# A weight's last row spread by matmuls, a bias loaded in place, reloads on another DMA queue, and program order at a seam

## The chip, the core and the metric

The kernel runs on one core of a Trainium2 chip. The metric is the device time of one execution in microseconds (us), the median of several runs. A core has TensorE (PE, with its weight loads shown apart as PEld), VectorE (DVE), ScalarE (ACT), GpSimd (POOL) and SyncE (SP). SP, ACT and POOL can issue DMAs, each on a queue of its own; the transfers themselves run on 16 DMA engines that the queues share.

## The reference: two half feed-forwards around a long convolution

The input x has 8 sequences of 2048 tokens with 256 channels. Three residual sub-layers follow one another:

```python
x = x + 0.5 * ffn(layernorm(x), w1, b1, w2, b2)
x = x + s4(layernorm(x), ...)
x = x + 0.5 * ffn(layernorm(x), w1, b1, w2, b2)

ffn(x):  relu(x @ w1 + b1) @ w2 + b2            # w1 is 256 x 1024, w2 1024 x 256
s4(x):   y = causal convolution of every channel along the 2048 tokens with its own kernel K
         r = x + y + x * D
         (r - mean(r)) / sqrt(var(r) + 1e-5) * ln_w + ln_b
```

Everything is float32. In the first and last layer norm of the list above (those ahead of `ffn`) there is no scale or shift.

## The kernel before

**Numbers in two parts.** A float32 product is made on PE as three matmuls of parts: each operand is split into a high part, rounded, and a low part, the rest. So w1 and w2 are kept as pairs `w1t[0], w1t[1]` and `w2t[0], w2t[1]`, and the layer's input as `xh, xl`.

**The last row and the bias.** A normalised row sums to zero over the 256 channels, so the last channel can be dropped: `load_weights` subtracts w1's last row from every row, and the place of row 255 takes the bias b1, with the input's channel 255 set to 1.0 (a memset of `xn`'s last column). To do that it loads w1 in four quarters of 256 columns (lines 163 to 167, on SP), then the last row and the bias, each broadcast to all 128 partitions (lines 168 and 169, 512 KB of written data each, on ACT's queue), then w2 in two halves (line 172, SP). Per quarter, DVE subtracts the last row (line 177), adds the bias through a column of the identity which is 1 on partition 127 only (line 178, recorded as the helper's line 117), ACT rounds the high part (182) and DVE subtracts for the low part (183). Partition p, slot d of `raw1` holds row 128 d + p, so row 255 is on partition 127.

**FFN sub-layers.** `sublayer` (line 819 on) runs a feed-forward over 64 groups of 256 tokens. A group has 8 steps, one for each 128 of the 1024 hidden columns: `up` makes six matmuls (line 802), ACT and DVE take the relu in two parts (lines 870 and 117), `down` makes six matmuls (line 812) three steps later. A generator `pre(g)` prepares the input of a group some steps ahead (load, statistics, root, norm, transposition into `xh`, `xl`), one stage per step; `post(g, po)` adds the result and stores it. The framework may change the order of instructions on an engine by its own planned times, unless an instruction is kept in program order. `sublayer` keeps ACT and DVE in program order in its lead-in (before the first matmul step) if it has work in `first`, or if the constant `MB` is set; `first` is `load_weights()` in sub-layer a and empty in b, and `MB = 0`.

Once split, the weights are also written to DRAM (lines 198 and 199), since the S4 block uses their place in SBUF (tags `wA`, `wB`) for its states.

**The S4 block.** The convolution runs over 32 batches of 8 channels, in groups `gr` 0 to 11. The last group but two (`gr` 9) is batches 26 and 27, then come 28 and 29, and 30 and 31. `states(gr)` (matmuls of line 984) makes the states between 128-token blocks, a recurrence on DVE or POOL carries them on, and `outputs(gr)` makes the result: for every batch it loads two `tz` (line 1036; a Toeplitz matrix of the convolution kernel from `kpad`) and two `ot` (line 1054) on SP, 256 KB each; ACT copies the input into two `uc` (1043); PE makes 16 matmuls of `tz` by `uc` (line 1059, 128 rows) and 32 of `ot` by the states (1068, 64 rows, in two halves c = 0, 1 that use different rows of the array); ACT evacuates the two results into `u` (1074). The tiles of these loads are borrowed from tags of the FFN stage (`xl`, `pl`, `x`, `xh`, `xn`), so a load starts when its tile is free.

**The seam.** After the last batch in the program stand the reload of w1 for sub-layer b (line 1147, eight pieces of 256 KB on SP, into `wb1`, tag `wA`), of w2 (line 1151, four pieces of 512 KB on SP, into `wb2`, tag `wB`), and the broadcasts of ln_w and ln_b on POOL's queue (line 1160). They are issued as soon as their tiles are free, so among the loads of the last batches: those of wb1 went out between 1039.45 and 1045.5, those of wb2 from 1074.67. Then `pre_b` starts: it loads the x of a group (line 1168, SP) into one of five `x` slots, adds ln_b on POOL, takes the statistics of the convolution's rows (`st_r`, `mv_r`), the root on ACT (`s_r`), the scaled difference `ys` (1184 on, recorded at the helper's line 117), adds it to x, and goes on with a second norm (`st_fb` to `nb_fb`, `xn`) and the transposition.

Of the kernel before, what the change touches and what calls it, by code (L numbers as in the profile page):

```python
# [10 lines left out]
F32 = mybir.dt.float32  # L11
F32R = mybir.dt.float32r
# [3 lines left out]
ALU = mybir.AluOpType  # L16
# [3 lines left out]
P = 128  # L20
# [23 lines left out]
def macaron_s4d_kernel(  # L44
# [17 lines left out]
    nc = tc.nc  # L62
    V = nc.vector
    A_ = nc.scalar
    G_ = nc.gpsimd

    B, L, H = x.shape
    N = c_re.shape[1]
    W = w1.shape[1]
# [4 lines left out]
    NDC = H // P  # L74
    NFC = W // P
    NTB = 2
# [5 lines left out]
    PINW = 1  # L82
    NZ = 1
    PINF = 0
    MB = 0
    PINT = 1
    XY = 4
    NU = NFC // 2
# [16 lines left out]
    wpool = ctx.enter_context(tc.tile_pool(name="wpool", bufs=1))  # L105
# [4 lines left out]
    def bank(tag, name):  # L110
        return ps.tile([P, 512], F32, name=name, tag=tag, bufs=BANKS[tag])

    def slot(tag, shape, name, dtype=F32):
        return work.tile(shape, dtype, name=name, tag=tag, bufs=BUFS[tag])

    def stt(o, a, s, b, op0, op1):
        return V.scalar_tensor_tensor(out=o, in0=a, scalar=s, in1=b, op0=op0, op1=op1)  # L117
# [4 lines left out]
    ident = const.tile([P, P], F32, name="ident")  # L122
# [27 lines left out]
    W1Q = [nc.sync] * 4  # L150
    W2Q = [nc.sync] * 2

    def load_weights():
        for _ in range(XL):
            yield
        q = W // 4
        raw1 = room[1][:, 0 : NDC * W].rearrange("p (i d f) -> p i d f", i=4, d=NDC)
        raw2 = room[1][:, NDC * W : NDC * W + NFC * H].rearrange("p (f m) -> p f m", m=H)
        last, bias = (
            room[1][:, NDC * W + NFC * H + i * W : NDC * W + NFC * H + (i + 1) * W] for i in range(2)  # L160
        )
        w2v = w2.rearrange("(fc p) m -> p fc m", p=P)
        for i in range(4):
            fs = slice(i * q, (i + 1) * q)
            W1Q[i].dma_start(
                out=raw1[:, i], in_=w1[:, fs].rearrange("(dc p) f -> p dc f", p=P)
            )
        nc.scalar.dma_start(out=last, in_=w1[H - 1].partition_broadcast(P))
        nc.scalar.dma_start(out=bias, in_=b1.partition_broadcast(P))
        for i in range(2):  # L170
            fs = slice(4 * i, 4 * i + 4)
            W2Q[i].dma_start(out=raw2[:, fs], in_=w2v[:, fs, :])
        for _ in range(7):
            yield
        for i in range(4):
            fs = slice(i * q, (i + 1) * q)
            V.tensor_sub(
                raw1[:, i], raw1[:, i], last[:, fs].unsqueeze(1).to_broadcast([P, NDC, q])
            )
            stt(raw1[:, i, NDC - 1], bias[:, fs], ident[:, P - 1 : P], raw1[:, i, NDC - 1], ALU.mult, ALU.add)  # L180
            hi = w1t[0][:, :, fs]
            A_.copy(hi, raw1[:, i])
            V.tensor_sub(w1t[1][:, :, fs], raw1[:, i], hi.bitcast(F32))
            yield
        for _ in range(NZ):
            yield
        for i in range(4):
            fs = slice(2 * i, 2 * i + 2)
            hi = w2t[0][:, fs, :]
            for ins in (  # L190
                A_.activation(hi, raw2[:, fs], AF.Copy, scale=0.5),
                stt(w2t[1][:, fs, :], raw2[:, fs], 0.5, hi.bitcast(F32), ALU.mult, ALU.subtract),
            ):
                if i < PINW:
                    tc.keep_in_program_order(ins)
            yield
        for i in range(2):
            nc.sync.dma_start(out=w1_dram[i], in_=w1t[i].bitcast(F32))
            nc.sync.dma_start(out=w2_dram[i], in_=w2t[i].bitcast(F32))
# [700 lines left out]
    xts = {}  # L900
# [45 lines left out]
    BL = 9  # L946
    xbuf = {}
    steps = {}

    BEHIND = [BH] * (len(PLAN) - 1) + [BL]  # L950

# [76 lines left out]
    def outputs(gr):  # L1028
        xs = states_of(gr)
        for p0, bt in batches(gr):  # L1030
            py, tzs, ucs, ots = [], [], [], []
            for c in range(2):
                tz = slot(TZS[gr >= LASTX][(2 * bt + c) % 3], [P, PB, P], f"tz{bt}_{c}")

                row = kpad[BCH * bt + c, 1:]
                nc.sync.dma_start(
                    out=tz,
                    in_=bass.AP(row.tensor, row.offset, [[1, P], [2 * KROW, PB], [1, P]]),
                )
                tzs.append(tz)  # L1040

                uc = slot("hx", [P, PB, P], f"uc{bt}_{c}")
                A_.copy(
                    uc.rearrange("p l (q m) -> p l q m", q=NQ),
                    u[:, :, BCH * bt + c : BCH * (bt + 1) : 2, :].rearrange("p q l m -> p l q m"),
                )
                ucs.append(uc)
            for ri in range(2):
                tag = OTS[gr >= LASTX][(2 * bt + ri) % 4]
                ot = (  # L1050
                    slot(tag, [P, PB, P], f"ot{bt}_{ri}") if tag
                    else xn.rearrange("p i (l m) -> p (i l) m", m=P)
                )
                nc.sync.dma_start(out=ot, in_=o_dram[bt][:, ri * PB * P : (ri + 1) * PB * P])
                ots.append(ot)
            for c in range(2):
                py.append(bank("h", f"py{bt}_{c}").rearrange("p (l m) -> p l m", l=PB))
                for l in range(PB):
                    nc.tensor.matmul(
                        py[c][:, l, :], ucs[c][:, l, :], tzs[c][:, l, :],  # L1060
                        start=(l == 0), stop=False, skip_group_check=True,
                    )

            for l in range(PB):
                for ri in range(2):
                    for c in range(2):
                        cs = slice(c * N, (c + 1) * N)
                        nc.tensor.matmul(
                            py[c][:, l, :], xs[cs, ri, p0 + l, :], ots[ri][cs, l, :],
                            start=False, stop=(l == PB - 1 and ri == 1), skip_group_check=True,  # L1070
                        )
            for c in range(2):

                A_.copy(
                    uo[:, :, bt, :, c::2], py[c].rearrange("p l (q m) -> p q m l", q=NQ)
                )

    def some(j0, j1):

# [51 lines left out]
        {"half": NG // 2, "tables": NG * 3 // 4},  # L1131
    )

    for gr in (1, 2, 3):
        states(gr)
    for gr in range(len(sizes)):
# [1 line left out]
        if gr and gr + AHEAD < len(sizes):  # L1138
            states(gr + AHEAD)


    wb1 = wpool.tile([P, 2, NDC, W], F32R, name="wb1", tag="wA")
    wb2 = wpool.tile([P, 2, NFC, H], F32R, name="wb2", tag="wB")
    for f in range(0, W, W // 4):
        fs = slice(f, f + W // 4)
        for i in range(2):
            nc.sync.dma_start(out=wb1[:, i, :, fs].bitcast(F32), in_=w1_dram[i][:, :, fs])
    for f in range(0, NFC, 4):
        fs = slice(f, f + 4)
        for i in range(2):  # L1150
            nc.sync.dma_start(out=wb2[:, i, fs].bitcast(F32), in_=w2_dram[i][:, fs])

    G_.memset(xn[:, :, H - 1 : H], 1.0)
    ys = wpool.tile([P, 2, NTB, H], F32, name="ys", tag="wE")


    lnw_sb = slot("e", [P, H], "lnw_sb")
    lnb_sb = slot("te", [P, H], "lnb_sb")
    for dst, src in ((lnw_sb, ln_w), (lnb_sb, ln_b)):
        nc.gpsimd.dma_start(out=dst, in_=src.partition_broadcast(P))  # L1160

    def pre_b(g):
        by_dma = g >= DMA_B
        for _ in range(0 if by_dma else XL):
            yield
        xt = xts[g] = slot("x", [P, NTB, H], f"xb_{g}")
        i0 = g * NTB
        nc.sync.dma_start(out=xt, in_=x1_dram[i0 : i0 + NTB].rearrange("i m h -> m i h"))
        G_.tensor_add(xt, xt, lnb_sb.unsqueeze(1).to_broadcast([P, NTB, H]))  # L1169
        uc = [uo[:, i // CQ, :, i % CQ] for i in range(P - 1 - i0, P - 1 - i0 - NTB, -1)]  # L1170
        mv = stats(uc, f"r{g}", PIN & 2)
        yield
        s = root(mv, f"r{g}")
        yield
        rs = rstds(mv, s, f"r{g}")
        yield
        y = ys[:, g % 2]
        for i in range(NTB):
            yb, lb = (t.rearrange("p (b h) -> p b h", h=BCH) for t in (y[:, i, :], lnw_sb))
            stt(yb, uc[i], mv[:, i, 0:1], lb, ALU.subtract, ALU.mult)  # L1180
        yield
        for i in range(NTB):
            ins = stt(xt[:, i, :], y[:, i, :], rs[:, i : i + 1], xt[:, i, :], ALU.mult, ALU.add)
            if PIN & 1:
                tc.keep_in_program_order(ins)
        yield
        return (yield from ffn_in(xt, f"b{g}", True, by_dma))
# [46 lines left out]
```

## Time and profile before

| | us |
|---|---|
| median of 3 runs | 1843.84 |
| lowest and highest | 1843.77, 1846.55 |
| the profiled execution | 1843.95 |
| its span in the trace | 1842.2 |
| last matmul of FFN a starts, first of the S4 block | 856.6, 860.8 |
| PE idle before the first transposition of FFN b begins | 1081.9 |
| first matmul of FFN b | 1094.31 |
| mean granted PE clock | 0.98 of full |

The page is one profiled execution. Its busy rows tell how long each engine worked; a row of the 40 slices has one digit for each 46 us, 9 for 90% and more. A line of a timeline has the start in us, the length in us, engine, source line, operation, what it writes `<-` what it reads, the shape, how many; in brackets how long the engine had been idle before, and what released it. Line numbers are those of the code above; line 117 is a helper that several places call. In a windows table each row is a stretch of time, with busy time and count per engine, then the granted PE clock, the mean busy share of the 16 DMA engines, and GB/s.

Section 6 of the page lists what DMAs took from issue to landing, in the median; four of its rows:

```profile
xa<-in_L_attn_x_dram SPq DMA_DIRECT2D x64, 256.0 KB, 2.9
...
tz<-kpad SPq DMA_DIRECT2D x64, 256.0 KB, 4.2
xb<-x_dram SPq DMA_DIRECT2D x64, 256.0 KB, 2.7
```

### The profile page before, as it was taken

Reading aid. Unit: us, or ns where it says so; the run is one execution under the profiler, and the core shown is the slowest. Engines: PE = TensorE matmul, PEld = TensorE weight load, DVE = VectorE, ACT = ScalarE, POOL = GpSimd, SP = SyncE. Lnnn points to the kernel's source line nnn. Section 1 sums busy time; section 2 is a strip of 40 time slices with the busy share of each in tenths; the row PEclk is TensorE's granted clock in tenths of the full one; section 3 lists DMA queues with packets and bytes.
Section 4 is the critical chain, followed back from the end, with each engine's and each line's share of the span. In section 5 each row is a group of like instructions: output and inputs, shape, how many; then the busy total and the mean of one; then the engine's idle time right before and its main releaser. Section 6 shows DMA issues by size and latency. Waiting matters only on the chain. (4 is left out here: it accounts for less than half of the span.)

```text
span 1842.2 us, 41540 instructions
## 1 busy us (share of the span) xinstructions
PE 1747.9 (95%) x15147; PEld 1715.8 (93%) x15147; DVE 1492.6 (81%) x4919; ACT 925.2 (50%) x2139; POOL 713.7 (39%) x964
## 2 busy tenths in 40 slices
PE   6999799998998999999989879999999999999999
PEld 5999799988998999998888879999999999999998
DVE  5999897888899867765999947888888888888875
ACT  4455334554655655553545425555555555555553
POOL 1116851888587414111778612222222222222220
PEclk9999899998999999999999979999999999999999
DMA  5112132787888933334878833333332333333332
GB/s 203 47 47 56 52 111 77 241 237 227 247 250 246 247 110 90 101 105 137 253 232 235 256 115 87 93 89 92 88 100 85 91 98 87 98 89 90 94 95 55
DMA packets 299696, 246.39 MB, mean 134 GB/s; under 512 B 169954, under 2 KB 242402, under 8 KB 298978
## 3 DMA queue, kind: packets, MB, share of 16 engines
q1 hardware_dynamic: 297456, 241.75, 45.2%
q8 instruction: 119, 1.95, 0.4%
q10 hardware_dynamic: 1266, 1.31, 0.2%
q0 software_dynamic: 768, 0.66, 0.2%
q14 instruction: 87, 0.71, 0.1%
HBM read 92.93 MB, written 111.15 MB: 111 GB/s over the span
## 5 line engine op out<-in xcount | busy, mean ns | idle before, releaser
L812 PE MATMUL po_a<-wa,hx_a 128*128 128x256 f32 x3072 | 457.1, 287 | 17.4 <-DVE hx_a L117 17.1
L802 PE MATMUL ph_a<-xh_a,wa 128*128 128x256 f32 x2048 | 460.2, 289 | 5.2 <-ACT xh_a L749 3.5
L802 PE MATMUL ph_b<-xh_b,wb 128*128 128x256 f32 x2048 | 443.2, 284 | 2.5 <-ACT xh_b L749 2.4
L812 PE MATMUL po_b<-wb,hx_b 128*128 128x256 f32 x3072 | 441.2, 283 | 0.3 <-DVE hx_b L117 0.3
L812 PEld LDWEIGHTS po_a<-wa,hx_a 128*128 128x128 f32 x3072 | 407.7, 194 | 23.4 <-DVE hx_a L117 22.4
L812 PEld LDWEIGHTS po_b<-wb,hx_b 128*128 128x128 f32 x3072 | 400.5, 192 | 0.5 <-DVE hx_b L117 0.5
L802 PEld LDWEIGHTS ph_a<-xh_a,wa 128*128 128x128 f32 x2048 | 361.3, 196 | 6.8 <-ACT xh_a L749 3.9
L802 PEld LDWEIGHTS ph_b<-xh_b,wb 128*128 128x128 f32 x2048 | 352.8, 193 | 3.6 <-ACT xh_b L749 3.0
L802 PE MATMUL ph_a<-xl_a,wa 128*128 128x256 f32 x1024 | 294.1, 290 | 23.4 <-DVE xl_a L751 20.6
L870 ACT ACTIVATE hx_b<-ph_b 128x256 fp32r<-128x256 f32 x512 | 191.6, 381 | 244.3 <-PE ph_b L802 226.6
L117 DVE SCALAR_TENSOR_TENSOR hx_a<-ph_a,hx_a 128x256 fp32r<-128x256 f32 x512 | 207.9, 412 | 127.7 <-ACT hx_a L870 126.6
L870 ACT ACTIVATE hx_a<-ph_a 128x256 fp32r<-128x256 f32 x512 | 189.0, 381 | 228.8 <-PE ph_a L802 213.6
L1169 POOL TENSOR_TENSOR xb<-xb,lnb_sb 128x512 f32<-128x512 f32 x64 | 84.0, 1315 | 523.3 <-DMA xb<-x_dram 384.4
L802 PE MATMUL ph_b<-xl_b,wb 128*128 128x256 f32 x1024 | 285.2, 284 | 0.0
L117 DVE SCALAR_TENSOR_TENSOR hx_b<-ph_b,hx_b 128x256 fp32r<-128x256 f32 x512 | 210.1, 414 | 57.3 <-ACT hx_b L870 51.7
L802 PEld LDWEIGHTS ph_a<-xl_a,wa 128*128 128x128 f32 x1024 | 201.2, 196 | 27.0 <-DVE xl_a L751 23.5
L733 POOL TENSOR_TENSOR xa<-xa,hb 128x512 f32<-128x512 f32 x64 | 85.5, 1336 | 362.4 <-ACT xn L701 328.0
L802 PEld LDWEIGHTS ph_b<-xl_b,wb 128*128 128x128 f32 x1024 | 197.4, 193 | 0.2 <-DVE xl_b L751 0.2
L701 ACT ACTIVATE xn<-xa,nb_fa,t_fa 128x255 f32<-128x255 f32 x128 | 69.7, 591 | 104.2 <-DVE nb_fa L117 82.2
L733 POOL TENSOR_TENSOR xb<-xb,hb 128x512 f32<-128x512 f32 x64 | 93.9, 1467 | 50.0 <-ACT xn L701 34.5
L701 ACT ACTIVATE xn<-xb,nb_fb,t_fb 128x255 f32<-128x255 f32 x128 | 69.9, 594 | 75.7 <-DVE nb_fb L117 72.0
L761 DVE COPY pl_b<-xn 128x512 uint16<-128x512 uint16 x62 | 42.7, 688 | 74.3 <-ACT xn L701 74.3
(264 smaller groups left out, 2773.2 us busy)
## 6 DMA issues: line engine op xcount, KB each, us to landing
xa<-in_L_attn_x_dram SPq DMA_DIRECT2D x64, 256.0 KB, 2.9
x_dram<-xa SPq DMA_DIRECT2D x64, 256.0 KB, 2.3
o<-u SPq DMA_DIRECT2D x32, 512.0 KB, 4.2
pv<-planes SPq DMA_DIRECT2D x32, 512.0 KB, 3.6
pt<-u SPq DMA_DIRECT2D x32, 512.0 KB, 3.3
tz<-kpad SPq DMA_DIRECT2D x64, 256.0 KB, 4.2
xb<-x_dram SPq DMA_DIRECT2D x64, 256.0 KB, 2.7
out_dram<-xb SPq DMA_DIRECT2D x64, 256.0 KB, 2.9
```

The source lines that it names most:

```text
L117: return V.scalar_tensor_tensor(out=o, in0=a, scalar=s, in1=b, op0=op0, op1=op1)
L701: A_.activation(dst, src, AF.Identity, bias=nb[:, i : i + 1], scale=rs[:, i : i + 1])
L733: G_.tensor_add(xt, xt, hb2.unsqueeze(1).to_broadcast([P, NTB, H]))
L761: copy(pl[:, w], xu[:, :, :, :, w])
L802: nc.tensor.matmul(ph, wt[wp][:, dc, fs], xp[:, dc, :], start=(n == 0), stop=(n == 3 * NDC - 1))
L812: nc.tensor.matmul(po[:, i, :], hp[:, tsl], wt[wp][:, fc, :], start=(fc == 0 and i == 0 and n == 0), stop=(fc == NFC - 1 and n == 2), skip ...
L870: last[A_] = A_.activation(hh, ph, AF.Relu)
L1169: G_.tensor_add(xt, xt, lnb_sb.unsqueeze(1).to_broadcast([P, NTB, H]))
```

## The change

At the start, the two broadcasts go. ACT loads w1's last row (4 KB) into one partition and the bias (4 KB) straight into partition 127, slot 1, of `raw1`. A row of ones is made on one partition, and PE multiplies it by the row in two matmuls of 512 columns, so that two PSUM banks hold the last row on every partition. Since partition 127 of slot 1 belongs to the bias now, each quarter of w1 is loaded in two pieces: slot 0 with 128 rows, and slot 1 with 127 rows. DVE subtracts the PSUM row from each piece; the addition of the bias goes.

At the seam, `late_loads` issues the broadcasts of ln_w and ln_b and two loads of 1 MB for `wb1` from ACT, right behind the evacuation of the first batch of `gr` 9 (batch 26); two of 1 MB for `wb2` follow the evacuation of batch 30. ln_w and ln_b lie in a slot of the tag `x`; in return the groups of sub-layer b rotate through the other `x` slots and two spare places, six in all. `MB = 1` keeps ACT and DVE in program order in sub-layer b's lead-in.

```diff
-    MB = 0
+    MB = 1
...
-        last, bias = (
-            room[1][:, NDC * W + NFC * H + i * W : NDC * W + NFC * H + (i + 1) * W] for i in range(2)
-        )
+        row = room[1][0:1, NDC * W + NFC * H : NDC * W + NFC * H + W]
+        ones = room[1][0:1, NDC * W + NFC * H + W : NDC * W + NFC * H + W + P]
+        V.memset(ones, 1.0)
+        nc.scalar.dma_start(out=row, in_=w1[H - 1 : H])
+        last = [bank("h", f"last{i}") for i in range(2)]
...
             W1Q[i].dma_start(
-                out=raw1[:, i], in_=w1[:, fs].rearrange("(dc p) f -> p dc f", p=P)
+                out=raw1[:, i, 0 : NDC - 1], in_=w1[0 : H - P, fs].rearrange("(dc p) f -> p dc f", p=P)
             )
-        nc.scalar.dma_start(out=last, in_=w1[H - 1].partition_broadcast(P))
-        nc.scalar.dma_start(out=bias, in_=b1.partition_broadcast(P))
+            W1Q[i].dma_start(out=raw1[0 : P - 1, i, NDC - 1], in_=w1[H - P : H - 1, fs])
+        nc.scalar.dma_start(
+            out=raw1[P - 1 : P, :, NDC - 1], in_=b1.rearrange("(o i f) -> o i f", o=1, f=q)
+        )
+        for i in range(2):
+            nc.tensor.matmul(
+                last[i], ones, row[:, i * 512 : (i + 1) * 512], start=True, stop=True
+            )
...
+            of = last[i // 2][:, i % 2 * q : (i % 2 + 1) * q]
             V.tensor_sub(
-                raw1[:, i], raw1[:, i], last[:, fs].unsqueeze(1).to_broadcast([P, NDC, q])
+                raw1[:, i, 0 : NDC - 1], raw1[:, i, 0 : NDC - 1],
+                of.unsqueeze(1).to_broadcast([P, NDC - 1, q]),
             )
-            stt(raw1[:, i, NDC - 1], bias[:, fs], ident[:, P - 1 : P], raw1[:, i, NDC - 1], ALU.mult, ALU.add)
+            V.tensor_sub(raw1[0 : P - 1, i, NDC - 1], raw1[0 : P - 1, i, NDC - 1], of[0 : P - 1])
...
-                A_.copy(
+                done = A_.copy(
                     uo[:, :, bt, :, c::2], py[c].rearrange("p l (q m) -> p q m l", q=NQ)
                 )
+            evacs.setdefault(gr, []).append(done)
...
+    def late_loads():
+        for i, src in enumerate((ln_w, ln_b)):
+            nc.scalar.dma_start(out=ln_sb[:, i], in_=src.partition_broadcast(P))
+        for i in range(2):
+            nc.scalar.dma_start(out=wb1[:, i].bitcast(F32), in_=w1_dram[i])
+        yield
+        for i in range(2):
+            nc.scalar.dma_start(out=wb2[:, i].bitcast(F32), in_=w2_dram[i])
+        yield
...
-    for f in range(0, W, W // 4):
-        fs = slice(f, f + W // 4)
-        for i in range(2):
-            nc.sync.dma_start(out=wb1[:, i, :, fs].bitcast(F32), in_=w1_dram[i][:, :, fs])
-    for f in range(0, NFC, 4):
-        fs = slice(f, f + 4)
-        for i in range(2):
-            nc.sync.dma_start(out=wb2[:, i, fs].bitcast(F32), in_=w2_dram[i][:, fs])
+        if gr == len(sizes) - 3:
+            ln_sb = slot("x", [P, 2, H], "ln_sb")
+            wb1 = wpool.tile([P, 2, NDC, W], F32R, name="wb1", tag="wA")
+            loads = late_loads()
+        if gr == len(sizes) - 1:
+            wb2 = wpool.tile([P, 2, NFC, H], F32R, name="wb2", tag="wB")
+        if gr in (len(sizes) - 3, len(sizes) - 1):
+            with tc.issue_after(evacs[gr][0].ins):
+                next(loads)
...
-    ys = wpool.tile([P, 2, NTB, H], F32, name="ys", tag="wE")
-    lnw_sb = slot("e", [P, H], "lnw_sb")
-    lnb_sb = slot("te", [P, H], "lnb_sb")
-    for dst, src in ((lnw_sb, ln_w), (lnb_sb, ln_b)):
-        nc.gpsimd.dma_start(out=dst, in_=src.partition_broadcast(P))
+    spare = wpool.tile([P, 4, NTB, H], F32, name="spare", tag="wE")
+    ys, xspare = spare[:, 0:2], spare[:, 2:4]
+    lnw_sb, lnb_sb = ln_sb[:, 0], ln_sb[:, 1]
...
-        xt = xts[g] = slot("x", [P, NTB, H], f"xb_{g}")
+        xt = xts[g] = xspare[:, g % 6 - 4] if g % 6 >= 4 else slot("x", [P, NTB, H], f"xb_{g}")
```

More of the change, by code (lines that the diff above doesn't have):

```diff
@@ L948, in macaron_s4d_kernel @@
     steps = {}
+    evacs = {}
     BEHIND = [BH] * (len(PLAN) - 1) + [BL]
@@ L1139, in macaron_s4d_kernel @@
             states(gr + AHEAD)
-    wb1 = wpool.tile([P, 2, NDC, W], F32R, name="wb1", tag="wA")
-    wb2 = wpool.tile([P, 2, NFC, H], F32R, name="wb2", tag="wB")
-    for f in range(0, W, W // 4):
-        fs = slice(f, f + W // 4)
-        for i in range(2):
-            nc.sync.dma_start(out=wb1[:, i, :, fs].bitcast(F32), in_=w1_dram[i][:, :, fs])
-    for f in range(0, NFC, 4):
-        fs = slice(f, f + 4)
-        for i in range(2):
-            nc.sync.dma_start(out=wb2[:, i, fs].bitcast(F32), in_=w2_dram[i][:, fs])
-    G_.memset(xn[:, :, H - 1 : H], 1.0)
-    ys = wpool.tile([P, 2, NTB, H], F32, name="ys", tag="wE")
-    lnw_sb = slot("e", [P, H], "lnw_sb")
-    lnb_sb = slot("te", [P, H], "lnb_sb")
-    for dst, src in ((lnw_sb, ln_w), (lnb_sb, ln_b)):
-        nc.gpsimd.dma_start(out=dst, in_=src.partition_broadcast(P))
+        if gr == len(sizes) - 3:
[7 more added lines that the diff above has]
+                next(loads)
+    G_.memset(xn[:, :, H - 1 : H], 1.0)
+    spare = wpool.tile([P, 4, NTB, H], F32, name="spare", tag="wE")
+    ys, xspare = spare[:, 0:2], spare[:, 2:4]
+    lnw_sb, lnb_sb = ln_sb[:, 0], ln_sb[:, 1]
     def pre_b(g):
```

## The prediction

> **What bounds the kernel now.** First the page's busy shares, to see which engine can set the end, and its 40 slices (46 us each), to see where that engine is not full.
>
> ```profile
> PE 1747.9 (95%) x15147; PEld 1715.8 (93%) x15147; DVE 1492.6 (81%) x4919; ACT 925.2 (50%) x2139; POOL 713.7 (39%) x964
> ...
> PE   6999799998998999999989879999999999999999
> ...
> PEclk9999899998999999999999979999999999999999
> ```
>
> PE is the bound. It is short of full in slice 0 (start of FFN a) and in slices 20 to 23 (end of the S4 block); slice 23 also has the one low clock digit, 7. From 1110 us to the end PE is full (0.3 us of idle before po_b in all), so nothing can be won in FFN b. The change edits just those two places, the start and the seam. The PE timeline shows the start:
>
> ```profile
> 14.01 1.22 PE L802 MATMUL ph_a<-xh_a,wa 128*128 128x256 f32 x4 [3.45 <-ACT xh_a L749]
> 19.19 0.58 PE L802 MATMUL ph_a<-xl_a,wa 128*128 128x256 f32 x1 [3.96 <-DVE xl_a L751]
> ```
>
> PE runs on from 19.19. What it waits for is DVE's program order: the timeline of DVE is almost gapless from 8.66 (first quarter of w1 landed) to xl_a at 18.46. Later, near 26.15, PE stops once more for 1.73. The windows view (columns: length; busy time and count of PE, PEld, DVE, ACT, POOL; granted clock; DMA share; GB/s) and the PE timeline show the seam:
>
> ```profile
> 1046.00:1049.00 3.00, 3.00 (x28) 2.76 (x27) 2.79 (x14) 1.75 (x3) 0.00 (x0) 1.00 1.05 346
> 1049.00:1053.00 4.00, 0.40 (x4) 0.21 (x2) 3.76 (x16) 0.61 (x1) 0.00 (x0) 0.70 1.08 323
> 1053.00:1058.00 5.00, 4.95 (x22) 4.75 (x23) 4.69 (x20) 0.62 (x1) 0.00 (x0) 0.50 0.72 225
> ...
> 1063.00:1068.00 5.00, 5.00 (x29) 4.60 (x28) 0.58 (x3) 0.62 (x1) 1.33 (x3) 0.50 0.43 95
> ```
>
> ```profile
> 1053.05 2.05 PE L1059 MATMUL py<-tz,uc 128*128 128x128 f32 x8 [3.65 <-DMA tz<-kpad]
> ...
> 1092.25 1.39 PE L740 MATMUL pt_b<-ident,xn 128*128 128x128 f32 x4 [10.37 <-ACT xn L701]
> ```
>
> Until batch 26 a batch takes 3.97 (16 tz matmuls 2.0, 32 ot matmuls 2.0). Batches 27 to 31 take 1046.26 to 1081.87, 35.6 where 5 x 3.97 = 19.9: 15.7 are lost. Then PE idles 10.37 for the first norm of FFN b.
>
> **The start, part by part.** Two broadcasts of 512 KB (the last row, the bias) leave ACT's queue. At 356 GB/s (DMA view, 8 to 12 us: share 1.09, so full) this 1 MB is 2.9 us of transfer; it stands beside SP's loads, and DVE is busy from its first quarter on, so it is worth at most 2.9, likeliest 1. PE's two new matmuls (row of ones by 512 columns) and the memset stand before 9.26, when PE first works: nothing; the 4 KB row is ACT's first DMA and has 6 us. DVE loses, per quarter, one 128x512 subtract (0.68) and one 128x256 multiply-add (0.48), and gets two 128x256 ones (0.48 each by that row): 0.2 each, two and a half quarters before xl_a: 0.5. (One operand now lies in PSUM; xl_a reads PSUM too, and its 128x512 takes 0.68, no more.)
>
> Against that: each quarter load (256 KB) is cut in a 128-row piece and a piece of **127 rows** of 1 KB, four more DMAs on SP. SP issues at 0.6 each (four took 2.49): 2.5, hidden under the transfers. How 127 rows are dealt to the 16 DMA engines no row of before shows. The nearest: in the DMA view of 140.2 to 144.0 a load into 2 partitions (256 pieces of 4 bytes) is
>
> ```profile
> q10 hardware_dynamic: 258, 0.00, 3.6%
> ```
>
> 258 packets = 256 + 2: two completions, so two engines, as many as partitions. The Trainium skill, "DMA: Bandwidth & Descriptors", section "Why a DMA increments its semaphore by 16 and not by 1", gives the general rule: the engine count is the largest number up to 16 that divides the outermost size on both sides, and 127 rows go through one engine. It speaks against the change, and the row agrees as far as it reaches; I take it.
>
> The price of a packet: 8 to 12 us moved 1452 packets of 1 KB on 16 engines in 4.0 us, 44 ns per packet and engine. On the engine that gets all the 127-row pieces, before the x rows of group 2 (DVE's program order has their statistics ahead of xl_a of group 0): 16 (xa of group 0) + 4 x (8 + 127) + 64 (w2) + 32 (xa of groups 1, 2) = 652 packets. 652 x 0.044 = 28.7, from 1.9: 30.6. Then statistics, aggregate, split of quarter 2 (0.74 + 0.23 + 0.66 by DVE's rows, and landing some 1.5): xl_a at some 33.5 instead of 18.46, so **+15**. The hole of 1.73 at 26.15 came from ACT, which stood at its five DMA issues while the x rows landed; these have landed before PE starts now: -1.7. Sum +13.5. FFN a is a steady pipeline in which PE waits little and its work is laid out in program order, so the delay reaches the end. Bounds: if that engine, with little beside it, reaches the rate of the weights' write in 8 KB rows (427 GB/s from 28 to 32 us), 1 KB takes 38 ns: 24.8 instead of 28.7, and the start +9.5. By a deal over all 16 engines: 2.9 at most won, -1.5 likeliest.
>
> **The seam: loads.** Removed: eight wb1 loads of 256 KB on SP at 1039.45 to 1045.5, four of wb2 (512 KB) at 1074.67. The tz of batch 27's second half was queued behind the eight; issued at 1046.24, it landed 6.7 later (tz loads: 4.2 in the median), and PE stopped 3.65. Moved: now two 1 MB loads of wb1, with ln_w and ln_b, are issued by ACT after the evacuation of batch 26 (about 1047.5), wb2's after that of batch 30. The changed program also interleaves the two halves of batches 27 and 28 on PE, which before came one after the other (16 unpaired 64-row matmuls at 0.11 instead of 0.064 each: 1.5 per batch and a half).
>
> Of the 15.7 lost: stall 3.65; unpaired 64-row matmuls 2 batches x 1.5 = 3; the rest, 9, is the clock of 0.50 from 1053 to 1068 and 0.70 until 1073. Here a rule and the trace differ: by "TensorE: Matmul & The Clock Gate", Part 1, one window of 3.4 us of busy PE brings the full rate back, so a stall would cost 1.7 in clock; here PE was over 95% busy for 15 us at half rate. I take the trace: with stall and unpaired matmuls gone, most of the 9 goes with them. By the rule the whole seam would give 3.65 + 3 + 1.7 = 8.4, by the row 15.7.
>
> What is late next: the transfers. From 1043.4 to batch 31 come 19 loads of 0.26 MB (tz, ot, xb), 0.26 of norm rows and 2.1 of wb1 = 7.3 MB; at 285 GB/s (window 1078 to 1082; 323 to 346 when fuller) 26 us, so about 1069, and PE ends batch 31 some 4 later, 1073.5 instead of 1081.87: **-8**. Bounds: 0 (wb1 in 8 KB rows beside the small loads makes a tz late again, the clock falls again) to -15. Waiting on ACT behind the wb1 issue are uc of batch 29 and the evacuation of batch 27: needed a batch later, so nothing. wb2 (2.1 MB, 9 us) is needed by the first down matmul, 1099 in before; hidden. ln_w is needed at 1084, lands by 1062; on POOL it landed in 3.5 and cost nothing either.
>
> **The seam: order.** In DVE's timeline from 1083.10 the chain of group 0 is broken by work of groups 1 and 2: four st_r (1.39), four mv_r (0.34 beside mv_fb), four ys (1.64), paired small ones (0.85). With program order they go behind; a root wait of 0.35 on ACT shows instead, and later groups' work falls in the wait for PE. xn 8.49 after st_r becomes some 6.3: **-2**, bounds 0 and -4. Two more x slots: FFN b does not wait for x; nothing.
>
> **Sum.** 1843.95 (the profiled execution; span 1842.2; 0.1 over the median 1843.84) + 13.5 - 8 - 2 = 1847.5; I say **1848**, as the small loads' delay behind wb1 is the likelier error at the seam.
>
> **Rivals.**
> *All sixteen engines* (17%): the pieces of 127 rows are spread like the others. Place: the w1 quarters at 5 to 20 us. Start -1.5, seam -10: 1832. It decides as soon as the start costs under 10. For it: only a 2-row load is seen in the trace. Against: the rule, and that row.
> *One engine, fast, and the whole seam* (17%): 38 ns a packet (+9.5), the seam near its full 13 + 2: 1838. For it: 16 busy engines shared one memory in the 44. Against: seam transfers stand at 0.9 to 1.08 share for tens of us.
> *The seam stalls again* (20%): wb1's long rows on ACT's queue against tz and ot: one stall of some 3 and half clock behind it; seam -3 in all: 1843.95 + 13.5 - 3 = 1854. For it: before's own stall came of such a load; ACT's loads of 64 KB (line 261) took 6.0 to 6.8 beside the 8 KB rows of 24 to 30 us, against 1.8 for the first of them. Against: wb1 now begins 8 us later, in two pieces, with four batches left, not five.
> *The forecast* (46%): 1848, its own range 1843 to 1853.
> That the loads are not where the change says is excluded by the instruction order on ACT.
>
> This kernel's measurement tells 0.2% (3.7 us) from no change. Slower: 0.25 of the forecast's 0.46, and the 0.20 of the stall: 0.45. Same: 0.17 and 0.03 of the fast engine: 0.20. Faster: 0.17 + 0.14 + 0.04 = 0.35. The range leaves out half of the first rival and the upper end of the third: 1832 to 1857.
>
> **What would show it.** Start: PE's steady run begins near 34, DVE waits for DMA between quarters, one queue's share stays near 1/16 while SP's loads land 6 us apart. If it begins near 18, the first rival holds. Seam: PEclk near 1.00 between 1053+13 and 1073+13, no stall over 1 before tz, batch 31's end 8 nearer to batch 26's; PE's idle before pt_b 8.4. Wrong if the shift of the start does not reach 1110's counterpart, or if a stall is back at batch 28 or 29.

## The result and the profile after

| | before | changed |
|---|---|---|
| median of 6 runs each | 1843.57 us | 1855.12 us |
| lowest and highest | 1841.16, 1846.55 | 1851.04, 1863.28 |
| ratio of the times, 95% interval | | 1.0068 [1.0046, 1.0090] |
| the profiled execution, its span | 1843.95, 1842.2 | 1863.28, 1861.4 |

The change makes the kernel slower by 11.5 us, 0.7%. Its profiled execution is the slowest of its six, 8 us over the median, so distances are read from its trace and totals from the medians. Line numbers of the changed code are 10 to 20 higher than those of the code above. The page's first rows again, of the changed kernel:

```profile
PE 1747.4 (94%) x15151; PEld 1711.9 (92%) x15151; DVE 1499.7 (81%) x4920; ACT 926.6 (50%) x2139; POOL 711.3 (38%) x962
...
PE   3999889988999899999999969999999999999998
...
PEclk9999999998999999999999979999999999999999
```

PE does the same work (1747.4 against 1747.9). Slice 0 fell from 6 to 3: the loss is at the start. Slice 23 fell from 7 to 6, but a slice is a fixed part of the span, and the seam lies elsewhere in it now; landmarks from the two timelines are better:

| landmark | before | changed | apart |
|---|---|---|---|
| PE's steady run begins (first matmul with xl of group 0) | 19.19 | 36.45 | +17.3 |
| DVE takes group 0's result in FFN a | 38.5 | 56.5 | +18.0 |
| DVE takes group 63's result in FFN a | 857.0 | 881.2 | +24.2 |
| PE ends batch 31 | 1081.9 | 1100.5 | +18.6 |
| DVE takes group 0's result in FFN b | 1108.0 | 1127.7 | +19.7 |
| span | 1842.2 | 1861.4 | +19.2 |

**The start.** PE's timeline of the changed kernel:

```profile
31.61 1.01 PE L812 MATMUL ph_a<-xh_a,wa 128*128 128x256 f32 x3 [23.56 <-ACT xh_a L759]
36.45 0.58 PE L812 MATMUL ph_a<-xl_a,wa 128*128 128x256 f32 x1 [3.83 <-DVE xl_a L761]
43.02 0.33 PE L284 MATMUL ptr<-ident,u 128*128 128x128 f32 x1 [1.29 <-DMA u<-n_L_attn_log_A_real_dram]
43.90 0.56 PE L812 MATMUL ph_a<-xh_a,wa 128*128 128x256 f32 x1 [0.55 <-DVE hx_a L117]
```

The DMA view of 10 to 22 us tells why (its GB/s row, one number for each 0.3 us, and its packets):

```profile
GB/s 20 24 24 75 328 75 20 24 24 24 20 24 24 20 24 24 20 24 24 24 20 24 24 85 328 65 24 20 24 24 20 24 24 24 20 24 24 20 24 24
DMA packets 542, 0.52 MB, mean 43 GB/s; under 512 B 34, under 2 KB 542, under 8 KB 542
```

For almost 6 us at a time 23 GB/s move, then a burst of 328. A piece of 127 rows of 1 KB takes 5.6 us at this rate, 44 ns a row; the burst is the 128-row piece of another quarter. The same view of 12 to 16 us alone, between two bursts, has the share of SP's queue:

```profile
q1 hardware_dynamic: 92, 0.09, 6.8%
```

With all engines full the share was 108.7% (kernel before, 8 to 12 us), and a sixteenth of that is 6.8%: one engine works. SP's own timeline shows that the loads behind were not even issued:

```profile
4.45 5.84 SPq L167 DMA_DIRECT2D u<-in_L_ffn_w_dram  x1
...
10.74 5.54 SPq L167 DMA_DIRECT2D u<-in_L_ffn_w_dram  x1
...
16.74 6.97 SPq L180 DMA_DIRECT2D u<-in_L_ffn_w_dram  x2
23.76 4.17 SPq L920 DMA_DIRECT2D xa<-in_L_attn_x_dram  x4
```

An issue that took 0.4 elsewhere takes 5.5 and more. The first two of these long issues end at 10.29 and 16.28, each about 0.6 before a burst: SP is held while a slow piece drains. x of groups 1 to 4 goes out at 23.76 instead of 6.19.

**The seam.** PE's timeline, and the windows view behind its stall:

```profile
1082.92 2.05 PE L1070 MATMUL py<-tz,uc 128*128 128x128 f32 x8 [6.99 <-DMA tz<-kpad]
...
1110.14 1.39 PE L750 MATMUL pt_b<-ident,xn 128*128 128x128 f32 x4 [9.62 <-ACT xn L711]
```

```profile
1083.00:1088.00 5.00, 5.00 (x34) 4.78 (x35) 4.80 (x12) 0.62 (x1) 2.56 (x2) 0.50 0.93 292
1088.00:1093.00 5.00, 5.00 (x56) 4.59 (x55) 1.97 (x8) 2.76 (x5) 0.00 (x0) 0.96 0.55 147
```

The stall has not gone. It moved from batch 27 to batch 28 and grew from 3.65 to 6.99. But the granted clock is back at 1088.4, 5.5 us after the stall's end. Before, it stayed at 0.50 for 18 us (the 0.70 of 1068 to 1073 is the mean of a window in which it changes); the first row is from the stretch at half clock, the second from behind it:

```profile
1068.00:1071.00 3.00, 3.00 (x17) 2.77 (x15) 0.00 (x0) 1.13 (x2) 3.00 (x3) 0.50 0.41 132
1071.00:1074.00 3.00, 3.00 (x41) 2.76 (x41) 0.00 (x0) 1.26 (x3) 0.56 (x1) 0.99 0.52 138
```

Batches 27 to 31 take 30.6 (1069.95 to 1100.5), before 35.6.

### The profile page after: what moved, and what is told of

Read it like the earlier page. It is cut to its first block, busy times and chain, and to the rows that moved or that the text cites. A ratio compares the mean times of both kernels' runs of the same rounds, so it can differ in the third digit from the quotient of the medians.

```text
span 1861.4 us, 41601 instructions
## 1 busy us (share of the span) xinstructions
PE 1747.4 (94%) x15151; PEld 1711.9 (92%) x15151; DVE 1499.7 (81%) x4920; ACT 926.6 (50%) x2139; POOL 711.3 (38%) x962
## 5 line engine op out<-in xcount | busy, mean ns | idle before, releaser
L812 PE MATMUL ph_a<-xh_a,wa 128*128 128x256 f32 x2048 | 460.2, 289 | 24.1 <-ACT xh_a L759 23.6
L1189 POOL TENSOR_TENSOR xb<-xb,ln_sb 128x512 f32<-128x512 f32 x44 | 57.1, 1298 | 370.4 <-DMA xb<-x_dram 245.2
L743 POOL TENSOR_TENSOR xb<-xb,hb 128x512 f32<-128x512 f32 x44 | 65.0, 1478 | 55.5 <-ACT xn L711 31.9
L1189 POOL TENSOR_TENSOR spare<-spare,ln_sb 128x512 f32<-128x512 f32 x20 | 25.9, 1294 | 157.8 <-DMA spare<-x_dram 86.8
```

The lines of the kernel that those rows point to most:

```text
L743: G_.tensor_add(xt, xt, hb2.unsqueeze(1).to_broadcast([P, NTB, H]))
L812: nc.tensor.matmul(ph, wt[wp][:, dc, fs], xp[:, dc, :], start=(n == 0), stop=(n == 3 * NDC - 1))
```

## The experiments

Twelve kernels ran, each over several rounds beside the kernel before.

| run | what it is | median | ratio to before, interval |
|---|---|---|---|
| e1 | changed, 127 rows as 112 + 15 | 1829.35 | 0.9924 [0.9912, 0.9937] |
| e2 | changed, 127 rows as 122 + 5 | 1838.21 | 0.9969 [0.9956, 0.9981] |
| e3 | before + changed start | 1861.41 | 1.0096 [1.0082, 1.0109] |
| e4 | before + changed seam | 1836.48 | 0.9961 [0.9948, 0.9975] |
| e5 | e1 + wb1 behind batch 30 | 1829.20 | 0.9923 [0.9908, 0.9938] |
| e6 | e1 + the two broadcasts | 1833.09 | 0.9939 [0.9922, 0.9955] |
| e7 | before + program order | 1843.24 | 0.9999 [0.9987, 1.0011] |
| e8 | before + paired matmuls | 1837.28 | 0.9965 [0.9951, 0.9978] |
| e9 | e5 + POOL's adds held back | 1829.52 | 0.9933 [0.9920, 0.9946] |
| e10 | e8 + program order | 1836.85 | 0.9971 [0.9960, 0.9982] |
| e11 | before + changed start as in e1 | 1835.60 | 0.9961 [0.9949, 0.9973] |
| e12 | e5 + the adds on DVE | 1829.34 | 0.9912 [0.9894, 0.9930] |

The kernel before had medians of 1841.88 to 1845.45 in these comparisons, so differences below some 2 us between runs of different rows are not told apart.

### How many engines a load gets (e1, e2)

```diff
-            W1Q[i].dma_start(out=raw1[0 : P - 1, i, NDC - 1], in_=w1[H - P : H - 1, fs])
+            for r0, r1 in ((0, 112), (112, P - 1)):        # e2: (0, 122), (122, P - 1)
+                W1Q[i].dma_start(out=raw1[r0:r1, i, NDC - 1], in_=w1[H - P + r0 : H - P + r1, fs])
```

> The changed kernel with each 127-row piece of w1 loaded as 112 and 15 rows; nothing else differs. Theory (all of the start's 18 us is 127 packets per piece on one DMA engine): the pieces now spread over 16 and 15 engines, PE's steady run begins at 18 to 20 us instead of 36.45, and the time is 1855 - 17 = 1837 to 1839. Rival (the loss comes from the start's other edits: eight or more issues on SP, DVE working from PSUM, the matmuls ahead of PE): SP now has twelve issues, PE begins later than 30 and the time stays at 1850 or more.

> The changed kernel with each 127-row piece loaded as 122 rows (2 x 61) and 5 rows. Theory (engines = largest number up to 16 that divides the rows): 61 packets on each of two engines; on the fullest engine 16 + 4 x (8 + 61 + 1) + 64 + 32 = 392 packets of 44 ns = 17.2 us from 1.9, PE's steady run begins at about 22 to 24, time 1840 to 1844. Rival (any count that isn't a multiple of 16 goes to one engine): 122 packets in a row, PE begins at 35 as with 127, time about 1855. Rival (rows that don't divide are dealt out as evenly as can be, and 127 was slow for another reason): as with 112 and 15.

PE's steady run began at 15.20 in e1 and at 21.47 in e2, against 36.45 with 127 rows. The first is from e1's timeline, the second from e2's:

```profile
15.20 0.58 PE L815 MATMUL ph_a<-xl_a,wa 128*128 128x256 f32 x1 [3.34 <-DVE xl_a L764]
```

```profile
21.47 0.58 PE L815 MATMUL ph_a<-xl_a,wa 128*128 128x256 f32 x1 [8.19 <-DVE xl_a L764]
```

The same bytes, in twelve DMAs instead of eight, and 21 us less. The count of rows decides: 122 rows (2 x 61) lie between, near the 22 to 24 worked out for two engines, and e2's DMA view of 7 to 9 us has 49 GB/s, about twice the 23:

```profile
q1 hardware_dynamic: 103, 0.10, 14.2%
```

"All on one engine" for every count that is no multiple of 16 and "dealt out evenly" are both out. The rule of the Trainium skill on which the prediction rested ("DMA: Bandwidth & Descriptors", section "Why a DMA increments its semaphore by 16 and not by 1": the largest number up to 16 that divides the rows) agrees at 127 and 122 rows, and 112 + 15 rows show no loss. Both kernels beat the time expected of them, e1 by 8 us; the next runs say by what.

### The two halves of the change apart (e3, e4, e11)

```diff
 # e3, against the kernel before (load_weights as changed); e11 with e1's split beside it
-        nc.scalar.dma_start(out=last, in_=w1[H - 1].partition_broadcast(P))
-        nc.scalar.dma_start(out=bias, in_=b1.partition_broadcast(P))
+            W1Q[i].dma_start(out=raw1[0 : P - 1, i, NDC - 1], in_=w1[H - P : H - 1, fs])
...
 # e4, against the changed kernel: the same lines the other way round
```

> The kernel before with the changed start alone (load_weights of the changed kernel, 127-row pieces); seam as before. Theory: the start carries through whole: 1843.6 + 17 to 18 = 1861. Rival (FFN a's slack or the longer lead lets a part be caught up): 1850 to 1857.

> The changed kernel with the start of before; seam loads on ACT's queue and program order stay. Theory (the seam gains 5 to 6 of the 35.6 us of batches 27 to 31 and 1 by order, FFN a's drift in the one profile was chance): 1843.6 - 6 = 1837 to 1839. Rival (the seam gains nothing beyond run-to-run change, and the start costs only 12): 1843 to 1845. A stall of PE before a tz matmul of batch 27 or 28 is expected in the trace by the theory, since wb1 still moves beside the last loads.

> The kernel before with the changed start alone, its 127-row pieces loaded as 112 and 15 rows. Theory (the start by itself gains what 1 MB less of transfers in front of x and w1 costs, about 7 by the difference of the runs with and without it): 1836 to 1838. Rival (the gain of 7 was partly the planner's other order in FFN a in that one program): 1839 to 1842.

The start alone costs 17.3 (1861.41 against 1844.09), carried through whole; the seam alone gains 7.6. Their sum is +9.7, the change +11.5. With its rows over 16 engines the same start gains 6.3 (1835.60 against 1841.88). So the start is a good edit spoilt by 127 rows: the difference between e3 and e11, each against its own runs of before, is 23.6, and that is what these rows cost. In e3's trace FFN a adds 2.3 to the start's delay, in the changed kernel's 6.2; DVE's order there is the planner's and differs, and one trace can't say how much of it is chance.

### What the broadcasts cost (e6)

```diff
+        for i, src in enumerate((w1[H - 1], b1)):
+            at = NDC * W + NFC * H + (2 + i) * W
+            nc.scalar.dma_start(out=room[1][:, at : at + W], in_=src.partition_broadcast(P))
```

> As the run with 112 and 15 rows, plus the two broadcasts of 512 KB of before on ACT's queue at the start, into room that nothing reads; 1 MB more to move, all else the same. Theory (the start gains by 1 MB less in front of x and w1: the first statistics begin at 3.6 instead of 6.2): the first statistics begin at 5.5 or later, PE's steady run at 17.5 to 19, time 1829.35 + 3 to 5 = 1832.5 to 1834.5. Rival (the gain is DVE's shorter work and another order of its instructions, the transfers are hidden): PE's steady run stays at 15.2, time 1829 to 1830.

PE's start came as the theory had it (18.60 against 15.20), and so did the median, 3.7 us over e1's, though two of e6's five runs (1828.24 and 1829.65) are no slower than e1's and the intervals overlap. The theory's way there was wrong: the first statistics still began at 3.60. There the broadcasts go out at 1.37 and 1.77, behind the 4 KB row; in the kernel before the first goes out at 0.74, together with x. The DMA view of 0 to 4 us of the kernel before shows what that does:

```profile
q10 hardware_dynamic: 94, 0.39, 39.1%
q1 hardware_dynamic: 51, 0.05, 4.9%
...
xa<-in_L_attn_x_dram SPq DMA_DIRECT2D x1, 256.0 KB, 5.4
```

ACT's queue (q10, rows of 4 KB) moved 0.39 MB while SP's (q1, rows of 1 KB) moved 0.05. x took 5.4 to land; without the broadcasts, in e1, 2.9. In e6 they go out 0.6 later and x is not delayed; there it is a piece of w1 that DVE waits for, 2.94, where in e1 no such wait shows.

### Clock, pairing, order and loads at the seam (e7, e8, e10)

```diff
-    MB = 0                                                        # e7, e10
+    MB = 1
...
+                    if bt >= 26:                                  # e8, e10: both matmuls of outputs()
+                        tc.keep_in_program_order(mm)
```

> The kernel before with program order in sub-layer b's lead-in alone. The prediction had 2 us for it. Theory by the traces of the changed kernels (PE idle before the first transposition 9.6 to 10.0 instead of 10.37): 0.5 to 1 faster, 1843 to 1843.5, not to be told from no change by the median; PE idle 9.6 to 9.8 in the trace. Rival (the order is worth its 2 us, and the new loads took some back): PE idle about 8.4, 1842.

> The kernel before, with PE's matmuls of batches 26 to 31 kept in the program's order, so that the two 64-row halves of a batch alternate; loads as before. Theory (PE's half clock of 15 us came from the unpaired 64-row matmuls, not from the stall): PE stalls 3 to 5 before batch 27's second tz as before, but the granted clock is back at 1.00 within 6 us of its end, batches 27 to 31 take 26 to 28 instead of 35.6, time 1834 to 1837. Rival (a stall at this place brings 15 us at half clock whatever the matmuls are): clock 0.50 for over 12 us, time 1840 to 1843.

> The kernel before with paired matmuls on PE in batches 26 to 31 and program order in sub-layer b's lead-in; weights and norm rows loaded as before. Theory (moving the loads to ACT's queue behind batch 26 brought nothing by itself, the changed seam gains by the pairing and the order): as fast as the changed kernel's seam alone (1836.48), 1835.5 to 1837.5. Rival (the moved loads are worth several us): 1839 or more.

e8 keeps every load of before, and its stall is longer (5.33). Its windows (the clock is the third number from the end):

```profile
1055.00:1058.00 3.00, 2.23 (x10) 2.04 (x12) 2.79 (x13) 0.09 (x1) 0.00 (x0) 0.50 1.09 343
1058.00:1061.00 3.00, 3.00 (x30) 3.00 (x32) 2.83 (x12) 0.53 (x1) 0.00 (x0) 0.50 0.49 133
1061.00:1064.00 3.00, 3.00 (x28) 2.65 (x28) 0.32 (x2) 2.02 (x4) 1.17 (x2) 0.88 0.46 113
1064.00:1067.00 3.00, 3.00 (x43) 2.88 (x40) 0.00 (x0) 1.67 (x4) 0.00 (x0) 1.00 0.92 284
```

The stall ends at 1055.77, the full clock is back 6.0 later, at 1061.7. So the 18 us at half clock came of the order of the matmuls behind the stall: PE counted as busy in both kernels, but unpaired, one matmul after the other used the same 64 of its 128 rows (at half clock one starts every 0.21 us in the kernel before, every 0.11 in e8). The other traces agree: from the end of the wait to the full clock it is 17.2 to 18.0 us in the four with the order of before (before, e3, e7, e11) and 3.2 to 6.5 in the ten whose halves alternate. (Why the clock is granted so is not shown.) Batches 27 to 31 take 28.5 instead of 35.6. Program order alone (e7) takes PE's idle time from 10.37 to 8.59, as the rival of that run had it; its median can't show so little. And e10, with pairing and order but every load as before, is as fast as the changed seam (1836.85 and 1836.48; the intervals of their ratios overlap). **The moved loads brought nothing in sum that can be measured; the seam's gain is the order of instructions, PE's above all**, which changed with them (why the framework pairs the halves once the loads stand elsewhere was not tried, nor the moved loads with the halves unpaired).

The tie is one of sums. In the one trace of each, batches 27 to 31 take 27.9 in e10 and 31.5 in e4, whose stall is longer (7.02 against 6.04). But e10's PE then idles 12.69 before FFN b's first transposition, e4's 9.76 and e8's 11.32: in e10 five adds on POOL, which had waited for loads, run beside the norm chain of group 0 on DVE and lengthen five of its operations, by 4.8 together. The POOL line and one of the DVE lines:

```profile
1070.38 6.69 POOL L1173 TENSOR_TENSOR xb<-xb,lnb_sb 128x512 f32<-128x512 f32 x5 [8.53 <-DMA wb<-w_dram]
1074.48 2.88 DVE L117 SCALAR_TENSOR_TENSOR xb<-ys,t_r,xb 128x256 f32<-128x256 f32 x2
```

In e7, without these adds beside them, the same two operations take 0.88 together. So program order in the lead-in gains 1.8 in e7's trace and nothing in e10's.

### What holds the seam once the stall is gone (e5, e9, e12)

```diff
         for i, src in enumerate((ln_w, ln_b)):                     # e5, e9, e12
             nc.scalar.dma_start(out=ln_sb[:, i], in_=src.partition_broadcast(P))
+        yield
         for i in range(2):
             nc.scalar.dma_start(out=wb1[:, i].bitcast(F32), in_=w1_dram[i])
-        yield
...
+        with ExitStack() as behind:                                # e9
+            if g < 2:
+                behind.enter_context(tc.issue_after(steps[len(sizes) - 1][-1].ins))
             G_.tensor_add(xt, xt, lnb_sb.unsqueeze(1).to_broadcast([P, NTB, H]))
...
-        G_.tensor_add(                                             # e12
+        (V if g < 3 else G_).tensor_add(
```

> As the run with 112 and 15 rows (1829.35), and the two 1 MB loads of wb1 move from behind batch 26's evacuation to behind batch 30's, ahead of wb2's; the norm rows stay. Theory (PE's stall of 7 us before batch 28's second tz, with the half clock behind it, is wb1's transfer in front of the last small loads): the stall goes, batches 27 to 31 take 20 to 23 us instead of 30, time 1819 to 1822. Rival A (the stall comes from tile release or SP's own queue): it stays, 1829. Rival B (wb1 is late for FFN b): PE waits for wb before its first ph_b matmul, 1825 or more.

> As the run with wb1 behind batch 30 (1829.2), and POOL's adds of ln_b for groups 0 and 1 are held back until the last group's recurrence on DVE has ended. Theory (a DVE operation beside one of these 128x512 adds on POOL takes 1.3 us instead of 0.28, two of them for each pair of adds; and the recurrence is what PE waits for once the stall is gone): no operation over 1 us in DVE's recurrence of the last group, PE's wait for xsE 3.04 falls to 0.5 to 1, batches 27 to 31 take 26.5, time 1826 to 1828. Rival (the two long operations are chance or come from DMA): they stay, or PE then waits for a later load, time 1829.

> As the run with wb1 behind batch 30 (1829.2), and the adds of ln_b for groups 0, 1 and 2 are made by DVE itself; POOL makes those of group 3 on. (In the run before, the adds were not held back: the first two were still at 1045.24 on POOL, beside DVE operations of 1.36 and 1.25.) Theory (two 128x512 adds on POOL cost DVE's recurrence 2.1 us where they meet): no operation of 1.2 us or more is left in the last group's recurrence but the add itself (0.7); the recurrence ends 1.5 us sooner after batch 27's start than the 23.1 of the run with wb1 behind batch 30; time 1827.5 to 1828.5. Rival (the long operations come from elsewhere, a transfer's writes for instance): operations of 1.2 us and more stay, time 1829 to 1830.

In e5 wb1 goes out at 1063.32 and is in time; the long stall before batch 28's second tz (7.08 in e1) becomes 0.97, so it was wb1's transfer that made this tz late. Batches 27 to 31 take 29.1 instead of e1's 30.9, not the 20 to 23 expected, and the time stays, since other waits stand behind the stall:

```profile
1044.26 0.71 PE L1082 MATMUL py<-ot,xsB 64*128 64x128 f32 x4 [1.08 <-DVE xsB L1037]
1045.93 2.05 PE L1073 MATMUL py<-tz,uc 128*128 128x128 f32 x8 [0.97 <-DMA tz<-kpad]
...
1061.05 2.06 PE L1082 MATMUL py<-ot,xsE 64*128 64x128 f32 x32 [3.04 <-DVE xsE L1037]
```

These two short waits cost the clock as a long one does (0.50 from 1045.6 to 1052.4). The length of a wait alone does not decide that: the clock stays at 1.00 through the 3.04 of the same trace, through 1.66 in e12 and through 0.62 and 1.27 in e9. Then PE needs `xsE`, the states of the last group, whose recurrence DVE ends at 1061. That recurrence ends 206 to 210 us after FFN a's last group in each of these traces (before 206.6, changed 208.9, e1 206.2, e5 209.1, e9 210.5, e12 207.0), and a batch and a half of matmuls, 6 us, must follow. Before, PE ended batch 31 at 224.9 on that scale, in the changed kernel at 219.3, in e5 at 215.2; by these numbers (206.6 and 6) an estimate of the least is 213, however early the loads are.

The recurrence can be delayed. e5's DVE and POOL timelines, where the operations of one step take 0.28 each:

```profile
1048.35 1.35 DVE L1034 TENSOR_TENSOR e<-xsE,wr_c 128x128 f32<-128x128 f32 x1
1049.62 1.35 DVE L1035 TENSOR_TENSOR te<-xsE,wi_c 128x128 f32<-128x128 f32 x1
```

```profile
1048.28 2.54 POOL L1192 TENSOR_TENSOR xb<-xb,ln_sb 128x512 f32<-128x512 f32 x2 [8.93 <-DMA xb<-x_dram]
```

In e9 the hold did not take: two adds were at 1045.24, a third at 1055.47, and beside them stood three long operations (1.36, 1.25, 1.37), two of them other steps than in e5. It does not test the cause, but the long operations follow the adds. In e12 the adds are DVE's and no operation over 0.7 is left: the cause is shown. The recurrence ended 20.2 after batch 27's start instead of 23.0. The time did not move (1829.34): two of the adds that DVE took over, those of groups 1 and 2, now stand in FFN b's lead-in ahead of xl_b (0.69, and 1.57 beside an add of POOL's), and PE waited 3.86 for xl_b, 1.64 in e5. The gain was given back a few us later.

## Why the prediction was right in direction and short in size

It said slower, 1848 in 1832 to 1857; measured were 1855.12. Its first rival, the load spread over all engines, is out for the change as it stands, and e1 is what it would have been. So the direction hung on one reading, that of the 127 rows, and this was right. The size owes something to luck: the forecast's own range, 1843 to 1853, was missed, and the third rival's sum, 1854, lies close only because a start put too small (+13.5 where +17.3 was measured) met a seam put too small (-3 where -7.6 was measured).

- **One engine, 44 ns a packet: right.** 23 GB/s and a sixteenth of the full share in the trace, and e1 and e2.
- **The step that was mis-sized: the start's sum, +13.5.** PE's steady run came 17.3 later, not 15. The prediction ended the transfers at 30.6 and put 3 us of work behind them. In the trace DVE goes on at 30.60, the same figure, but released by ACT's part of w2 (DVE idle 14.18) and not by x, and 5.1 us of its program order stand before xl_a: five splits of weights, two subtractions, two statistics. The blocked loads had also blocked their processing; the term left out was DVE's backlog, 2.1 us.
- **The hole, -1.7: wrong.** It was to close since x had landed by then. But ACT stood at its five DMA issues again (37.93 to 42.96), now beside the writing of the weights to DRAM, and 1.29 + 0.55 remain. With the backlog this is 3.9 of the 4.5 between +13.5 and +18.0.
- **Carried through FFN a: right** (e3: +17.3 of the median), and in the one trace with 6 more.
- **Broadcasts worth 1, at most 2.9: too low.** They had cost x 2.5 us of landing, and e11's start gains 6.3; e6 puts some 3.5 of it on the two broadcasts (3.4 in PE's start, 3.7 in medians that are not clear of each other). The rest, DVE's shorter work and x ahead of everything, was not separated.
- **The seam's loads, -8: half right, for another reason.** Batches 27 to 31 gained 5.0. The stall was to go with the loads' new place, and that failed: it came back at batch 28, which the prediction had named as a sign of being wrong, and twice as long, where the third rival had some 3. What paid was the term set down as 3 us, pairing (1.5 a batch comes out of 32 unpaired matmuls, not of the 16 written there): with it the half clock after a stall lasts 3.2 to 6.5 us and not 18. The prediction had 15 of 0.50 and a rest of 0.70. Taking the trace against the skill's 3.4 us (page "TensorE: Matmul & The Clock Gate", Part 1) was right for the order of before and wrong as a price of a stall: with the halves alternating, half of 3.2 to 6.5 is lost, 1.6 to 3.3, near the 1.7 by the rule.
- **What is late next: right for the change, wrong behind it.** The prediction named the transfers, and in the changed kernel a tz was late. Once that is out of the way, it is DVE's recurrence (e5, e12).
- **The order, -2: right alone** (e7: 1.8 in the trace; in e10 beside the pairing nothing), 0.75 in the changed kernel, where two DVE operations of 0.16 took 1.11 and 0.98 while POOL added (1106.90 to 1109.39). That and more is given back in FFN b's first group: PE ran at half clock for 7.0 us from its first matmul, before for 4.0.
- **wb2, ln_w, six x slots at nothing: right**; no wait for them shows.

In sum, by the medians of e3 and e4, +17.3 and -7.6 were measured where +13.5 and -10 were predicted: both terms erred to the slower side.

The best version found is e1, the change with its 127 rows split in 112 and 15: 0.9924 of before. e5 and e12 equal it.

## What to carry to other kernels

Before a tile is cut short by one row, count its rows' divisors: 127 rows cost some 23 us here, 112 + 15 nothing that shows, and everything on the queue behind pays as well. When a stall ends in a stretch of low clock, look at the matmuls in it: if two halves of the array could alternate, the order of instructions can be worth more than the transfer that caused the stall, as here. And before a stall is priced as a gain, find the next thing the engine would wait for, also on an engine that the stall itself had been covering.

## What the runs showed of the hardware

- A load of 1 KB rows lost against one of 4 KB rows issued at the same time on another queue: in the first 4 us of the kernel before 94 packets on ACT's queue carried 0.39 MB, 51 on SP's 0.05 MB, and a 256 KB load took 5.4 instead of 2.9 (e1).
- A DVE operation that reads two SBUF operands beside a POOL add of 128x512 takes about 1.0 longer (0.28 becomes 1.25 to 1.37), for each of POOL's adds once (changed, e5, e9). This fits what the Trainium skill says of a port pair that DVE and GpSimd lock for a whole instruction ("SBUF — State Buffer", section "SBUF: two separate sides"); e12 takes the adds away, and the long operations go.
- PE at over 95% busy did not bring the clock back where its 64-row matmuls ran one half after the other: 0.50 for 17.2 to 18.0 us after a stall in four traces (before, e3, e7, e11); with the halves alternating 3.2 to 6.5 us in ten.
- What a wait costs in clock can't be told from its length: 1.08 and 0.97, 0.7 apart, brought 0.50 in e5, and 3.04 later in the same trace did not.
